# Three weight tiles for four in an expert's gate and up, and a down projection over 112 and 64 rows

## The chip, the cores and the metric

The kernel runs on one core of a Trainium2 chip. The metric is the device time of one execution in microseconds; the time before is the median of three runs, 1116.88 us (1115.35 to 1118.17). All data is float32.

## The reference

A transformer block with attention and a mixture of experts, on an input of 4 batches x 512 tokens x 256 features. Only the second half matters here; cut to it:

```python
h = layernorm(x) * (1 + cb) + sb                      # 2048 tokens x 256
scores = softmax(h @ gate.T)                          # 64 experts
# of 8 groups of experts the best 3 are kept, then the best 6 experts of a token
slot = expert * 96 + min(position_in_expert, 95)      # each expert has 96 places
buf[slot] = h[token]                                  # 64 x 96 x 256
g = einsum("ech,emh->ecm", buf, Wg)                   # Wg, Wu: 64 x 176 x 256
u = einsum("ech,emh->ecm", buf, Wu)
out = einsum("ecm,ehm->ech", silu(g) * u, Wd)         # Wd: 64 x 256 x 176
y = sum over a token's 6 places of out * weight
x = x + gb * (y + shared_expert(h))
```

So each of 64 experts takes a block of 96 tokens by 256 features through two matrices of 176 x 256 (gate and up), multiplies silu of one with the other, and goes back through one of 256 x 176.

## The kernel before

The kernel first computes attention (some 860 us), then routes each token and scatters its row, with its six weights, into the places of its experts in device memory (`slots_d`). The last stage, from about 916 to 1085 us, goes through the 64 experts; it is the only one that the change touches.

**Loads.** `load_pair(j)` (L719 to L727) fetches the weights of experts 2j and 2j+1: `wgu`, 128 partitions (one half of the features each time, index k) by expert, k, gate or up, and 176 columns; and `wd`, 88 partitions by expert, half m (2 x 88 = 176 rows of the down projection) and 256 columns, in two DMAs, of 80 and of 8 partitions. All are issued by SyncE (L722, L725, L726), three DMAs for a pair. `PAIRS` = 9 pairs of buffers exist; nine pairs are asked for ahead of the stage, and in the stage `load_pair` of a later pair is called after the down projection of an even expert, when its buffers come free. `load_group` (L733) fetches the tokens' rows `xe` of two experts, 96 partitions, through ScalarE's queue (the first four through SyncE's).

**One expert.** `features(e)` transposes the block of 96 x 256 in two halves (L825), and VectorE copies the result to `xT` (L827): 128 features by half and 96 tokens. `up(e)` makes gate and up: for gate and up, two tiles m of 88 weight columns, two halves k of the contraction, thus eight products with 96 streamed columns (L836), all into one PSUM bank. ScalarE takes silu of the gate (L839) into `act`, 88 partitions by m and token; VectorE multiplies it by the up half (L884). `down(e)` contracts those 88 rows twice (m = 0, 1) against `wd`, 256 streamed columns, into 96 x 256 (L847). ScalarE scales each token's row by its weight (L849, tile `oe`, six buffers), and GpSimd issues an indirect DMA that adds the rows to a sum in device memory (L850). There are four such sums (`NACC`); `sum_of(e)` picks one in turn, and from expert 48 (`EARLY`) only three of them, as the first is read early. DMAs into one sum wait for one another.

**Order.** The engines' programs follow the order in which the code issues them. The loop at L877 issues for each e: `up(e)`, `features(e+1)`, VectorE's product of expert e, and then `down(e-1)`; so TensorE has gate and up of expert e, the transposes of e+1, and the down projection of e-1, before gate and up of e+1. `weights_of` (L735 to L746, small VectorE operations on `xe`) is called every second expert, and from expert 56 VectorE also adds the first sum into the result (L869, L872).

**After the experts.** The shared expert of the last batch (`shared`, L755, L762) and its down projection (L768) run on TensorE while SyncE loads the three remaining sums (L909) as soon as they are complete. The last products (L957) add what a token gets from places that several tokens share, and the result is written out.

Earlier lines that are used for comparison: L136, L231 (projections of q, k and v), L267 and L327 (transposes), L422 (the router's product of 128 weight columns with 64 streamed columns), L526 (a transpose with 64 weight columns), L610 (modulation: four weight columns), L619 (transposes of four rows).

Of the kernel before, what the change touches and what calls it, by code (L numbers as in the profile page):

```python
# [8 lines left out]
F32 = mybir.dt.float32  # L9
I32 = mybir.dt.int32  # L10
U32 = mybir.dt.uint32
AF = mybir.ActivationFunctionType
# [5 lines left out]
P = 128  # L18
B, T, D = 4, 512, 256
NT = B * T  # L20
KC = D // P
# [7 lines left out]
E, M, CAP, TOPK = 64, 176, 96, 6  # L29
EG, TOPG = 8, 3  # L30
EPG = E // EG
MC, MP = 2, 88
MS = 352
MS_CHUNKS = [(0, 128), (128, 128), (256, 96)]
GA, SB, CB, GB = 0, 1, 2, 3
# [11 lines left out]
DW = 80  # L47
# [6 lines left out]
def adaln_attention_moe(ctx: ExitStack, tc: tile.TileContext, x, wq, wk, wv, wo, qkw, rope,  # L54
                        gate, wgu, wd, sgu, sd, c, wmod, out):
    nc = tc.nc
# [6 lines left out]
    def bank(tag):  # L63
        return psum.tile([P, 512], F32, tag=tag, name=f"ps_{tag}")
# [113 lines left out]
    with ExitStack() as att:  # L178
# [30 lines left out]
        def attention_input(b, pool=None, i0=0, n=NI, tag="tr"):  # L209

            pool = pool or rt
            xn = pool.tile([P, n, D], F32, tag=f"xn{i0}", name="xn")
            at = statistics(pool, b, i0, n)
            if n < NI:
                yield
            normalized(xn, b, *at, i0)
            yield
            for k in range(KC):
                nc.vector.tensor_scalar(hT[:, k, b * T + i0 * P:b * T + (i0 + n) * P], transposed(xn, k, tag),
                                        caT[:, k, b:b + 1], saT[:, k, b:b + 1], ALU.mult, ALU.add)  # L220
            yield
# [129 lines left out]
        second = {}  # L351
# [225 lines left out]
        halves = [attention_input(0, mp, i, 2, tag) for i, tag in ((0, "tr"), (2, "av"))]  # L577
# [4 lines left out]
        for j in range(4):  # L582
            for k in range(KC):
                nc.tensor.matmul(ps[:, j * B:(j + 1) * B], wm[:, k, j * P:(j + 1) * P], sil[:, k, :],
                                 start=(k == 0), stop=(k == KC - 1))
# [62 lines left out]
        for u in range(-HG, NU + 2):  # L648
            p, s, a, t = u + HG, u, u - 1, u - 2
# [58 lines left out]
    work = ctx.enter_context(tc.tile_pool(name="work", bufs=3, reuse_waits="tile"))  # L708
    held_weights = ExitStack()
    wexp = held_weights.enter_context(tc.tile_pool(name="w_exp", bufs=PAIRS, reuse_waits="tile"))  # L710

    sgu_sb = ffn.tile([P, KC, 2, MS], F32, name="sgu_sb")
    nc.sync.dma_start(out=sgu_sb, in_=sgu)
# [4 lines left out]
    pairs, groups = {}, {}  # L718

    def load_pair(j):  # L720
        a = wexp.tile([P, 2, KC, 2, M], F32, tag="wgu", name="wgu")
        nc.sync.dma_start(out=a, in_=wgu[2 * j:2 * j + 2].rearrange("e p k g m -> p e k g m"))  # L722
        d = wexp.tile([MP, 2, MC, D], F32, tag="wd", name="wd")
        src = wd[2 * j:2 * j + 2].rearrange("e p c d -> p e c d")
        nc.sync.dma_start(out=d[:DW], in_=src[:DW])  # L725
        nc.sync.dma_start(out=d[DW:], in_=src[DW:])  # L726
        pairs[j] = a, d  # L727

    def load_group(j, eng=nc.scalar):

        xe = work.tile([CAP, XB, ROW], F32, tag="xe", name="xe", bufs=XBUFS)
        groups[j] = [xe]
        return eng.dma_start(out=xe, in_=slots_d[j * XB * CAP:(j + 1) * XB * CAP, :].rearrange("(e c) r -> c e r", c=CAP))  # L733

    def weights_of(j):  # L735
        xe, = groups[j]
        w = work.tile([CAP, XB, TOPK], F32, tag="w", name="w", bufs=4)
        ids = expert_id[:CAP, j * XB:(j + 1) * XB].unsqueeze(2).to_broadcast([CAP, XB, TOPK])
        nc.vector.tensor_tensor(w, xe[:, :, ID0:ID0 + TOPK], ids, ALU.is_equal)
        nc.vector.tensor_mul(w, w, xe[:, :, W0:W0 + TOPK])  # L740
        w1 = work.tile([CAP, XB], F32, tag="w1", name="w1", bufs=4)
        nc.vector.tensor_reduce(w1, w, AX.X, ALU.add)
        nc.vector.tensor_tensor(w1, w1, low[:, j * XB:(j + 1) * XB], ALU.max)
        to = work.tile([CAP, XB], I32, tag="to", name="to", bufs=4)
        nc.vector.tensor_tensor(to, xe.bitcast(I32)[:, :, TOK], low_i[:, j * XB:(j + 1) * XB], ALU.max)
        groups[j] += [w1, to]  # L746
# [27 lines left out]
    def rows(t, b):  # L774

        return t[b * T:(b + 1) * T, :].rearrange("(p i) d -> p i d", p=P)
# [22 lines left out]
    for j in range(PAIRS):  # L799
        load_pair(j)  # L800
# [14 lines left out]
    def sum_of(e):  # L815

        return e % NACC if e < EARLY else 1 + e % (NACC - 1) if e < E - 1 else 2

    xTs, acts = {}, {}

    def features(e):
        xe = groups[e // XB][0]
        ps = bank("tr")
        for k in range(KC):
            nc.tensor.transpose(ps[:, k * CAP:(k + 1) * CAP], xe[:, e % XB, k * P:(k + 1) * P], ident[:CAP, :CAP])  # L825
        xTs[e] = work.tile([P, KC, CAP], F32, tag="xT", name="xT", bufs=2)
        nc.vector.tensor_copy(xTs[e].rearrange("p k c -> p (k c)"), ps[:, :KC * CAP])  # L827

    def up(e):
        a, xT = pairs[e // 2][0], xTs.pop(e)  # L830
        gu = bank("mm")
        guv = gu[:MP, :2 * MC * CAP].rearrange("p (g m c) -> p g m c", g=2, m=MC)
        for gi in range(2):
            for m in range(MC):
                for k in range(KC):
                    nc.tensor.matmul(guv[:, gi, m, :], a[:, e % 2, k, gi, m * MP:(m + 1) * MP], xT[:, k, :],  # L836
                                     start=(k == 0), stop=(k == KC - 1))
        act = acts[e] = work.tile([MP, MC, CAP], F32, tag="act", name="act", bufs=2)
        nc.scalar.activation(act, guv[:, 0], AF.Silu)  # L839
        return guv  # L840

    def down(e):
        d, act = pairs[e // 2][1], acts.pop(e)
        _, w1, to = groups[e // XB]
        po = bank("av")
        for m in range(MC):
            nc.tensor.matmul(po[:CAP, :D], act[:, m, :], d[:, e % 2, m, :], start=(m == 0), stop=(m == MC - 1))  # L847
        oe = work.tile([CAP, D], F32, tag="oe", name="oe", bufs=6)
        nc.scalar.activation(oe, po[:CAP, :D], AF.Copy, scale=w1[:, e % XB:e % XB + 1])  # L849
        nc.gpsimd.indirect_dma_start(out=y_d[sum_of(e)],  # L850
                                     out_offset=bass.IndirectOffsetOnAxis(ap=to[:, e % XB:e % XB + 1], axis=0),
                                     in_=oe, in_offset=None, compute_op=ALU.add)
# [4 lines left out]
    def load_shared_slots(eng, first, hi, step):  # L857
        eng.dma_start(out=o95[first:hi:step, :], in_=y_d[sum_of(first)][NT + first:NT + hi:step, :])
# [6 lines left out]
    def fold():  # L865

        for b in range(B):
            t = first_sums.pop(b)
            nc.vector.tensor_mul(t, t, gates(b))  # L869
            yield  # L870
            xb = x_sb[:, b * NI:(b + 1) * NI, :]
            nc.vector.tensor_add(xb, xb, t)  # L872
            yield

    weights_of(0)
    features(0)
    for e in range(E + 1):  # L877
        if e < E:
            if e % XB == 0 and 0 < e and e // XB + XBUFS - 1 < E // XB:
                load_group(e // XB + XBUFS - 1)  # L880
            guv = up(e)
            if e + 1 < E:
                features(e + 1)
            nc.vector.tensor_mul(acts[e], acts[e], guv[:, 1])  # L884
            if e % XB == XB - 1 and e + 1 < E:
                weights_of(e // XB + 1)
        if e >= 1:
            down(e - 1)
            if e % 2 == 0 and e // 2 + PAIRS - 1 < E // 2:
                load_pair(e // 2 + PAIRS - 1)  # L890
        if e == EARLY + 2:
            for b in range(B):
                first_sums[b] = wexp.tile([P, NI, D], F32, tag="wgu", name="first")
                nc.sync.dma_start(out=first_sums[b], in_=rows(y_d[0], b))
            folding = fold()
            load_shared_slots(nc.sync, 0, EARLY, NACC)
        if e > EARLY + 7:
            next(folding, None)
# [49 lines left out]
    for b in range(B):  # L948
        banks, to = kept if b == B - 1 else places(("av", "mm"), 2)
        w = NI // len(banks)  # L950
# [8 lines left out]
        for lo in range(0, NI, n):  # L959
            o = own[2][b][:, lo:lo + n, :]  # L960
# [63 lines left out]
```

## Time and profile before

| | |
|---|---|
| time, median of three runs | 1116.88 us |
| the profiled execution's time | 1117.43 us |
| its span, first to last instruction | 1115.7 us |
| mean granted TensorE clock | 0.992 |
| TensorE busy, share of the span | 97% |
| TensorE weight loads busy | 69% |
| VectorE, ScalarE, GpSimd busy | 58%, 40%, 37% |
| expert stage, first gate product to last down product | 917 to 1074 us |
| gate and up, L836: instructions, mean length | 1024, 250 ns |
| down, L847: instructions, mean length | 256, 383 ns |
| accumulating DMAs, L850: issue, median time to landing | 1.4 us, 7.7 us |
| DMA in 940 to 1040 us | 285 to 305 GB/s |

The page of the profile shows one execution. A row of a group gives line, engine, operation, the tiles written and read with their shapes, the count, the busy time in us and the mean length of one in ns, then the idle time before it and what ended it. For a matrix product the shape is rows x columns of the weight tile, then the operand that streams. "PEld" is the loading of weight tiles, which the profile lists beside the products. A row of waits reads: engine and operation, what it waited for, us in total, how often, the longest. A row of the timeline reads: start, length, engine, line, operation, tiles, shapes, how many were merged, and in brackets the idle time before. Ends of TensorE's products are modelled, so its starts say more than its lengths.

### The profile page before, as it was taken

The numbers are of one execution on the slowest core, as the hardware profiler recorded it, in microseconds if no ns is written. First come the engines' busy times: TensorE is split into PE (matmuls) and PEld (weight loads), VectorE is DVE, ScalarE is ACT, GpSimd is POOL, SyncE is SP. The second block draws the span as 40 slices with busy tenths as digits, with TensorE's granted clock in tenths as the row PEclk, the third lists the DMA queues.
The fourth block names the chain that finished last, engine by engine and source line by source line (L and its number), as shares of the span: only waits on it lengthen the run. The fifth ranks groups of instructions, "written<-read, shape, count | busy, mean of one in ns | idle before, by whom it ended". The sixth has DMA issues, their size and how long they took to land. (4 is left out here: it accounts for less than half of the span.)

```text
span 1115.7 us, 15635 instructions
## 1 busy us (share of the span) xinstructions
PE 1085.4 (97%) x5700; PEld 767.0 (69%) x5700; DVE 643.9 (58%) x1571; ACT 448.0 (40%) x741; POOL 417.7 (37%) x578
## 2 busy tenths in 40 slices
PE   9999999999999999999899999999999989999997
PEld 4567676667666766666667667666768659999966
DVE  5655655556667555567665556676544833444467
ACT  2553435344434453544444444535352412333320
POOL 3232223132223464323145632223562374565550
PEclk9999999999999999999999999999999998999999
DMA  5646404223101131110102220200122869999965
GB/s 191 227 114 183 161 12 149 78 84 104 57 20 63 49 112 67 40 56 21 57 30 97 77 88 9 68 1 30 60 89 88 229 221 244 303 297 289 264 140 200
DMA packets 67349, 130.20 MB, mean 117 GB/s; under 512 B 6564, under 2 KB 38852, under 8 KB 67144
## 3 DMA queue, kind: packets, MB, share of 16 engines
q1 hardware_dynamic: 48416, 102.49, 28.6%
q0 software_dynamic: 11776, 19.67, 7.1%
q10 hardware_dynamic: 7080, 7.04, 2.2%
q8 instruction: 45, 0.74, 0.3%
q14 instruction: 32, 0.26, 0.1%
HBM read 90.23 MB, written 38.94 MB: 116 GB/s over the span
## 5 line engine op out<-in xcount | busy, mean ns | idle before, releaser
L244 DVE TENSOR_REDUCE ss<-sq 128x4 f32<-128x512 f32 x128 | 87.2, 685 | 163.3 <-ACT sq L243 163.3
L145 POOL TENSOR_SCALAR rmsv<-ss 128x8 f32<-128x8 f32 x64 | 12.6, 198 | 448.2 <-DVE ss L244 448.2
L289 PE MATMUL ps_sc<-qT,kT 128*128 128x512 f32 (+3 forms) x512 | 158.1, 446 | 0.1
L314 PEld LDWEIGHTS ps_av<-v,es 128*128 128x128 f32 x1280 | 152.4, 192 | 3.0
L314 PE MATMUL ps_av<-v,es 128*128 128x129 f32 x1280 | 153.5, 275 | 0.0
L271 ACT COPY qT<-ps_tr 128x512 f32<-128x512 f32 x64 | 37.4, 585 | 267.1 <-PE ps_tr L267 267.1
L289 PEld LDWEIGHTS ps_sc<-qT,kT 128*128 128x128 f32 x512 | 87.2, 190 | 53.3 <-issue 31.3
L231 PE MATMUL ps_mm<-wk,hT 128*128 128x512 f32 x256 | 120.7, 594 | 0.7 <-ACT tokq L242 0.7
L231 PE MATMUL ps_mm<-wq,hT 128*128 128x512 f32 x256 | 120.6, 593 | 0.0
L231 PE MATMUL ps_mm<-wv,hT 128*128 128x512 f32 x256 | 120.6, 593 | 0.0
L338 PE MATMUL ps_mm<-wo,attnT 128*128 128x256 f32 x512 | 113.9, 380 | 4.8 <-DVE v L256 4.8
L850 POOL DMA_INDIRECT y_d<-oe,to x64 | 95.3, 1489 | 62.1 <-ACT oe L849 45.8
L292 ACT ACTIVATE es<-ps_sc 128x512 f32<-128x512 f32 (+1 forms) x192 | 99.9, 526 | 37.7 <-PE ps_sc L289 31.3
L338 PEld LDWEIGHTS ps_mm<-wo,attnT 128*128 128x128 f32 x512 | 96.9, 190 | 24.9 <-issue 6.7
L357 POOL DMA_INDIRECT slots_d<-row,to x96 | 95.5, 995 | 34.4 <-issue 15.5
L146 POOL TENSOR_TENSOR rmsr<-rmsv,mhalf 128x8 f32<-128x8 f32 x64 | 105.5, 1648 | 5.3
L836 PEld LDWEIGHTS ps_mm<-xT,wgu 128*88 128x88 f32 x1024 | 96.7, 161 | 9.1 <-issue 1.1
L836 PE MATMUL ps_mm<-xT,wgu 128*88 128x96 f32 x1024 | 98.2, 250 | 1.2 <-issue 0.7
L252 DVE TENSOR_TENSOR tokq<-tokq,rmsr 128x512 f32<-128x512 f32 x64 | 45.2, 706 | 89.6 <-POOL rmsr L146 89.6
L231 PEld LDWEIGHTS ps_mm<-wk,hT 128*128 128x128 f32 x256 | 48.3, 190 | 62.9 <-issue 57.2
L242 ACT COPY tokq<-ps_mm 128x512 f32<-128x512 f32 x64 | 37.5, 586 | 124.4 <-PE ps_mm L231 124.4
L294 ACT ACTIVATE es<-es 128x1280 f32<-128x1280 f32 x64 | 81.3, 1271 | 2.0
(207 smaller groups left out, 1502.3 us busy)
## 6 DMA issues: line engine op xcount, KB each, us to landing
wgu<-in_wgu SPq DMA_DIRECT2D x32, 704.0 KB
wd<-in_wd SPq DMA_DIRECT2D x32, 320.0 KB
y_d<-blank SPq DMA_DIRECT2D x4, 2304.0 KB
wq<-in_wq SPq DMA_DIRECT2D x16, 512.0 KB
wk<-in_wk SPq DMA_DIRECT2D x16, 512.0 KB
wv<-in_wv SPq DMA_DIRECT2D x16, 512.0 KB
wo<-in_wo SPq DMA_DIRECT2D x16, 512.0 KB
slots_d<-blank SPq DMA_DIRECT2D x1, 6528.0 KB
```

What stands on the lines that cost most here:

```text
L146: nc.gpsimd.tensor_tensor(r, v, mhalf[:, :n], ALU.pow)
L231: nc.tensor.matmul(ps, hT[:, k, lo:lo + P], weights[n, name][:, k, :], start=(k == 0), stop=(k == KC - 1))
L244: nc.vector.tensor_reduce(ss[:, j * HG:(j + 1) * HG], sq.rearrange("p (h d) -> p h d", d=HD), AX.X, ALU.add)
L252: nc.vector.tensor_mul(tv, tv, r[:, j * HG:(j + 1) * HG].unsqueeze(2).to_broadcast([P, HG, HD]))
L289: nc.tensor.matmul(ps[:, at:at + T - j * P], kT[:, j * P:(j + 1) * P], qT[:, j * P:], start=True, stop=True)
L292: nc.scalar.activation(es[:, base[js[0]]:base[js[0]] + at], ps[:, :at], AF.Tanh, scale=HD ** -0.5 / SOFTCAP)
L294: nc.scalar.activation(es[:, :1280], es[:, :1280], AF.Exp, scale=SOFTCAP)
L314: nc.tensor.matmul(pv[:, i2, :], es[:, lo:lo + P], v_tiles[n % 2][:, j, h, :], start=(j == 0), stop=(j == i))
L338: nc.tensor.matmul(ps[:, :D], attnT[n][:, h, i * P:(i + 1) * P], weights[n, "o"][:, h, :], start=(h == 0), stop=(h == HG - 1))
L357: d = nc.gpsimd.indirect_dma_start(out=slots_d, out_offset=bass.IndirectOffsetOnAxis(ap=to, axis=0), in_=rows, in_offset=None)
L836: nc.tensor.matmul(guv[:, gi, m, :], a[:, e % 2, k, gi, m * MP:(m + 1) * MP], xT[:, k, :], start=(k == 0), stop=(k == KC - 1))
L850: nc.gpsimd.indirect_dma_start(out=y_d[sum_of(e)], out_offset=bass.IndirectOffsetOnAxis(ap=to[:, e % XB:e % XB + 1], axis=0), in_=oe, in_o ...
```

## The change

Gate and up take the 176 columns as 112 + 64. Three weight tiles are used for four: gate's first 112 columns, a joined tile of 128 columns with the last 64 of gate and the last 64 of up, and up's first 112. The joined tile does not lie together in `wgu`, so VectorE copies those columns of a pair of experts to a new tile `wgc` (`join(j)`, two buffers): once ahead of the loop for pair 0, then after the multiplications of every even expert for the pair that comes next.

The products land in three pieces of 96 columns of the bank; the middle one has gate's last 64 on partitions 0 to 63 and up's last 64 on 64 to 127. ScalarE takes silu in two operations, VectorE multiplies in two. The second part of `act` goes to partitions 0 to 63 for even experts and 64 to 127 for odd ones (`second_chunk`).

The down projection contracts 112 rows, then 64 rows. The weights for it are two tiles: `wd1`, 112 partitions for both experts, and `wd2`, 128 partitions, the even expert's 64 rows above the odd one's. The array in device memory is as before (88 rows by two halves), so `wd1` takes 80 and 8 rows of the first half and 24 of the second, and `wd2` 64 rows of the second half, for each expert: five DMAs of rows of 256 elements, where there were two of rows of 512. With `wgu`, a pair is loaded in six DMAs.

```diff
+MA, MB = 112, 64
...
     def load_pair(j):
         a = wexp.tile([P, 2, KC, 2, M], F32, tag="wgu", name="wgu")
         nc.sync.dma_start(out=a, in_=wgu[2 * j:2 * j + 2].rearrange("e p k g m -> p e k g m"))
-        d = wexp.tile([MP, 2, MC, D], F32, tag="wd", name="wd")
+        d1 = wexp.tile([MA, 2, D], F32, tag="wd1", name="wd1")
+        d2 = wexp.tile([P, D], F32, tag="wd2", name="wd2")
         src = wd[2 * j:2 * j + 2].rearrange("e p c d -> p e c d")
-        nc.sync.dma_start(out=d[:DW], in_=src[:DW])
-        nc.sync.dma_start(out=d[DW:], in_=src[DW:])
-        pairs[j] = a, d
+        nc.sync.dma_start(out=d1[:DW], in_=src[:DW, :, 0])
+        nc.sync.dma_start(out=d1[DW:MP], in_=src[DW:, :, 0])
+        nc.sync.dma_start(out=d1[MP:], in_=src[:MA - MP, :, 1])
+        for e2 in range(2):
+            nc.sync.dma_start(out=d2[second_chunk(e2), :], in_=src[MA - MP:, e2, 1])
+        pairs[j] = [a, d1, d2]
+
+    def join(j):
+
+        a = pairs[j][0]
+        c = work.tile([P, 2, KC, 2, MB], F32, tag="wgc", name="wgc", bufs=2)
+        nc.vector.tensor_copy(c.rearrange("p e k g m -> p (e k g) m"), a.rearrange("p e k g m -> p (e k g) m")[:, :, MA:])
+        pairs[j].append(c)
+
+    def second_chunk(e):
+
+        return slice(e % 2 * MB, (e % 2 + 1) * MB)
...
     def up(e):
-        a, xT = pairs[e // 2][0], xTs.pop(e)
+        (a, _, _, c), xT = pairs[e // 2], xTs.pop(e)
         gu = bank("mm")
-        guv = gu[:MP, :2 * MC * CAP].rearrange("p (g m c) -> p g m c", g=2, m=MC)
-        for gi in range(2):
-            for m in range(MC):
-                for k in range(KC):
-                    nc.tensor.matmul(guv[:, gi, m, :], a[:, e % 2, k, gi, m * MP:(m + 1) * MP], xT[:, k, :],
-                                     start=(k == 0), stop=(k == KC - 1))
-        act = acts[e] = work.tile([MP, MC, CAP], F32, tag="act", name="act", bufs=2)
-        nc.scalar.activation(act, guv[:, 0], AF.Silu)
-        return guv
+        g, both, u = (gu[:, at * CAP:(at + 1) * CAP] for at in range(3))
+        halves = ((g[:MA, :], a[:, e % 2, :, 0, :MA]), (both, c[:, e % 2].rearrange("p k g m -> p k (g m)")),
+                  (u[:MA, :], a[:, e % 2, :, 1, :MA]))
+        for o, w in halves:
+            for k in range(KC):
+                nc.tensor.matmul(o, w[:, k, :], xT[:, k, :], start=(k == 0), stop=(k == KC - 1))
+        act = acts[e] = work.tile([P, 2, CAP], F32, tag="act", name="act", bufs=2)
+        second = second_chunk(e)
+        nc.scalar.activation(act[:MA, 0, :], g[:MA, :], AF.Silu)
+        nc.scalar.activation(act[second, 1, :], both[:MB, :], AF.Silu)
+        return (act[:MA, 0, :], u[:MA, :]), (act[second, 1, :], both[MB:, :])
 
     def down(e):
-        d, act = pairs[e // 2][1], acts.pop(e)
+        (_, d1, d2, _), act, second = pairs[e // 2], acts.pop(e), second_chunk(e)
         _, w1, to = groups[e // XB]
         po = bank("av")
-        for m in range(MC):
-            nc.tensor.matmul(po[:CAP, :D], act[:, m, :], d[:, e % 2, m, :], start=(m == 0), stop=(m == MC - 1))
+        nc.tensor.matmul(po[:CAP, :D], act[:MA, 0, :], d1[:, e % 2, :], start=True, stop=False)
+        nc.tensor.matmul(po[:CAP, :D], act[second, 1, :], d2[second, :], start=False, stop=True)
...
+    join(0)
     weights_of(0)
     features(0)
     for e in range(E + 1):
...
-            guv = up(e)
+            products = up(e)
             if e + 1 < E:
                 features(e + 1)
-            nc.vector.tensor_mul(acts[e], acts[e], guv[:, 1])
+            for g, u in products:
+                nc.vector.tensor_mul(g, g, u)
+            if e % 2 == 0 and e + 2 < E:
+                join(e // 2 + 1)
```

## The prediction

> **What bounds the kernel now.** I read the page first (TensorE busy 97% of the span), then the table of TensorE's waits in the expert stage, then its order of work there, then the end of the stage on GpSimd. The waits of PE from 900 to 1085 us:
>
> ```profile
> PE ps_tr L825 <- DMA xe<-slots_d: 2.3, 1, 2.3
> PE ps_mm L836 <- issue: 0.7, 1, 0.7
> PE ps_mm L836 <- DVE xT L827: 0.5, 1, 0.5
> PE ps_tr L768 <- DVE hs L762: 0.2, 1, 0.2
> ```
>
> There is no wait for a weight tile (`wgu`, `wd`) and none for an activation. So through 64 experts the PE order itself sets the pace. One expert of the timeline (start, length, engine, line; lengths overlap because ends are modelled, so read the starts):
>
> ```profile
> 950.62 0.33 PE L825 MATMUL ps_tr<-ident,xe 96*128 96x96 f32 x2
> 950.79 1.03 PE L847 MATMUL ps_av<-wd,act 88*96 88x256 f32 x4
> 951.47 1.51 PEld L836 LDWEIGHTS ps_mm<-xT,wgu 128*88 128x88 f32 x16
> 951.66 1.49 PE L836 MATMUL ps_mm<-xT,wgu 128*88 128x96 f32 x16
> 952.98 0.33 PE L825 MATMUL ps_tr<-ident,xe 96*128 96x96 f32 x2
> ```
>
> Starts give 0.17 us for the transposes, 0.87 for the down projection (4 x 216 ns), 1.32 for gate and up (16 x 82.5 ns): 2.36 per expert. A matrix product of float32 is two instructions here (16 for 8 products). The loads run beside the products, at the same pace.
>
> The end of the kernel hangs on something else. ScalarE's last result tile, then GpSimd's last accumulating DMAs:
>
> ```profile
> 1072.87 0.47 ACT L849 ACTIVATE oe<-ps_av,w 96x256 f32<-96x256 f32 x1 [0.57 <-PE ps_av L847]
> 1074.34 1.41 POOL L850 DMA_INDIRECT y_d<-oe,to  x1 [0.30 <-issue]
> 1076.06 1.41 POOL L850 DMA_INDIRECT y_d<-oe,to  x1 [0.30 <-issue]
> 1078.40 1.41 POOL L850 DMA_INDIRECT y_d<-oe,to  x1 [0.93 <-DMA y_d<-oe,to]
> ```
>
> The last tile is ready at 1073.34 and goes out at 1078.40: 5.1 us late, against 0.3 in mid-stage. Accumulations into one sum wait for one another, and from expert 48 there are three sums instead of four. So TensorE is followed by a short backlog, and a small slowing of TensorE would first only empty it.
>
> **Gate and up.** Twelve instructions replace sixteen, but the weight tiles grow from 88 columns to 112 and 128, while 96 columns are streamed as before. If streaming set the pace, 4 x 82.5 ns x 64 = 21 us would go. The trace has a row for the opposite case, the router's product: 128 weight columns, 64 streamed.
>
> ```profile
> 871.48 1.00 PE L422 MATMUL ps_mm<-gate_sb,hT 128*128 128x64 f32 x8
> 871.49 0.86 PEld L422 LDWEIGHTS ps_mm<-gate_sb,hT 128*128 128x128 f32 x7 [0.24 <-issue]
> ```
>
> (0.86 - 0.19) / 6 = 112 ns from load to load: loads set the pace there. A load of 88 columns lasts 157 ns (median, L836), one of 128 columns 192 (L422): 0.875 ns per column, so a load of 112 paces at 112 - 14 = 98 ns, one of 88 at 77 (below 82.5, which is why streaming rules now). New gate and up: 8 x 98 + 4 x 112 = 1232 ns of loads, less the first, which hides under the down projection's 216 ns, plus the last stream of 82: 1.216 us. Saving 0.104 us per expert, 6.7 us in all, not 21.
>
> Here the Trainium skill (TensorE: Matmul & The Clock Gate, Part 3, The mechanism) says otherwise: a weight load overlaps products in flight only if it goes to another row group. Then each instruction would pay load plus stream (80), 16 x 157 = 2.51 us now and 8 x 178 + 4 x 192 = 2.19 after: 20 us gained. The trace shows 16 loads of all 128 rows in 1.51 us beside 16 products in 1.49, so I take the row.
>
> **Down.** Still four instructions of 256 streamed columns, 216 ns each; fewer or more rows change nothing in the count. But the second product contracts 64 rows. The skill (TensorEngine Tiling (Array Packing), Key Properties) says that a change of tiling mode drains TensorE, and lists 64x128 as a mode of its own. Every expert would change twice: into it within the down projection, and back for the next gate and up. What a change costs is to be seen early in the trace, where L610 has a weight tile of four columns between full ones:
>
> ```profile
> 21.76 0.38 PE L267 MATMUL ps_tr<-ident,tokk 128*128 128x128 f32 x2
> 22.07 3.60 PE L610 MATMUL ps_av<-wm,sil 128*4 128x512 f32 x8
> 25.60 1.98 PE L231 MATMUL ps_mm<-wv,hT 128*128 128x512 f32 x4
> 27.42 1.88 PE L231 MATMUL ps_mm<-wq,hT 128*128 128x512 f32 x4
> 25.59 0.30 PEld L231 LDWEIGHTS ps_mm<-wv,hT 128*128 128x128 f32 x2 [0.86 <-issue]
> ```
>
> In: L267's last product starts at 21.76 + 0.38 - 0.27 = 21.87, the next is due 0.11 later, and comes at 22.07: +0.09. Out: L610's last starts at 25.08, the next is due at 25.51 and comes at 25.60: +0.09; its load began only then, uncovered, and the four products take 1.98 instead of 1.88: +0.10. So a change costs 93 ns plus the first load, which is no longer hidden. The four-row transposes (L619, 31.8 us) show the same both ways. Against it stands L526, with 64 weight columns:
>
> ```profile
> 845.04 0.60 PE L526 MATMUL ps_tr<-ident,share 128*64 128x128 f32 x4
> 845.48 0.60 PE L327 MATMUL ps_tr<-ident,attn 128*128 128x128 f32 x4
> ```
>
> 0.44 us for four, no gap, no loss. That is a transpose in float32, for which the same page (Restrictions) excludes column tiling, so it need not be a mode at all. Bounds for the two changes: nothing (as L526) and, as L610, 93 + 84 (a load of 96 columns) and 93 + 98 = 368 ns. I take 368: L526 alone is of the other kind. Net per expert 368 - 104 = +264 ns; times 64, less the last way out, +16.7 us at TensorE. By L526 it is -6.7.
>
> **What follows at the end.** At 2.62 us per expert the backlog goes: with weight loads over, three accumulations take 6.2 to 7.7 us (1058.28, 1064.47, 1072.12, 1078.40), 2.2 per expert. During the loads it is 9.1 for three (1042.43 to 1051.49), 3.0, but expert 48 then comes at about 1052, and the last pair of weights, issued at 1038, lands near 1046. So the last accumulation goes out 16.7 - 4.8 = 11.9 us later. The final products (L957) wait 1.5 us for DMA now; TensorE alone was ready at 1092.9. It arrives 16.7 later less the 2.3 us that L768 waits for `hs` (held up on VectorE by a sum that will now come early relative to it): 1107.3, against 1106.4 for the DMA side. So +12.9 us, +15.2 if that wait stays.
>
> **Beside the path.** VectorE copies 512 columns per pair (nearest rows, copies of 128x512 from PSUM at L256 and L328: 0.69; it can't be dearer by much) and multiplies twice (two of about 0.25 for 0.34); ScalarE activates twice (about +0.17). In 921 to 1040 us they are busy 46 and 39 of 119 us, and the `xT` copy, next on VectorE behind this copy, waits 84 us in 60 times for TensorE, 1.4 each: cover for 0.69. Without it a pair would lose up to 0.7 us. The copy reads the next pair's `wgu` one expert early; queued behind a late one would be `xT`, then TensorE. But the last pair landed at 1046.3 and is used at 1067.0, the tightest of all. `wd` goes in runs of 1 KB for 2 KB: packets of these sizes take 46 and 84 ns (medians), (352 x 46 - 176 x 84) / 16 = 0.09 us per pair on each DMA engine, 2 us over 22 pairs, within those 20.7. SyncE issues six DMAs per pair for three, some 1.05 us more of the 4.7 us per pair, where it is busy 1.04. All this I cost at nothing.
>
> **Sum.** 1117.43 + 12.9 = 1130.3 for the profiled execution, which lies 0.55 above the median: **1129.8 us**. Its own range, from drains of 300 ns to the `hs` wait kept and the copy sometimes uncovered, is 1123 to 1136.
>
> **Rivals.** (1) No drain for 64 rows (0.18): faster side. TensorE gains 6.7 us, but accumulations come four apart in 9.1 to 9.6 us when they queue (1025.79 to 1035.40, 1028.99 to 1038.07), 2.3 to 2.4 per expert, slower than TensorE's 2.25: the gain partly becomes backlog. Between 0 and -6.7, -3.5: 1113.4. It decides if the two changes cost under 104 + 4.8 / 64 x 1000 = some 180 ns, half of L610's. (2) The drain without uncovered loads (0.10): 186 - 104 = 82 ns, 5.2 us, nearly all of it taken by the backlog: 1117 to 1120. (3) Streaming sets the pace after all, and no drain: -21 us at TensorE, stopped by the accumulations at about 2.3 per expert, again near 1113; L422 speaks against it, and I count it within (1).
>
> Drain in full: 0.72. A difference under 0.3% (3.4 us) can't be told from no change here. Slower: 0.72 + half of (2) = 0.77; same: half of (2) and half of (1), 0.14; faster: half of (1), 0.09. The range that holds 8 in 10 runs from 1113.5 (half of rival 1 left out) to 1136.
>
> **What would show it.** Right: in the stage PE's two 64-row products start about 0.39 us after the 112-row ones instead of 0.22, the first gate load starts after, not with, the last down product; loads at 98 and 112 ns; 2.6 us per expert; POOL's lag 0.3 at the end. Wrong: loads under the last down product, 2.25 us per expert, and a lag over 5 us; or PE waits for `act`, `xT` or `wgu`, which I excluded.

## The result and the profile after

The change made the kernel slower: a median of 1148.72 us (1144.8 to 1154.45, four runs) against 1116.12 (1109.82 to 1118.17, four runs) for the kernel before, a ratio of **1.0306 [1.0245, 1.0367]** (ratios here and below are estimated from all runs of both kernels; the two medians alone give 1.0292). The forecast was 1129.8, with a range to 1136. The profiled execution of the changed kernel took 1144.8 us, with a span of 1143.0; it is the fastest of the four, so the median lies 3.9 us above what is accounted for here. (The granted clock was 0.988 in it and 0.981 to 0.983 in the others; every trace here has the clock at full or at half, so that 0.007 less over 1145 us is an estimated 16 us more at half, which could cost up to 8 us; the other three have no profile to show it.)

In the changed kernel the transposes are on L841, gate and up on L853, silu on L856 and L857, the down projection on L864 (112 rows) and L865 (64 rows), the result tile on L867, its accumulation on L868. The weights of a pair are issued on L723 (`wgu`) and L727 to L731, the token rows on L749, the loads of the first sum on L916, and its addition to the result is on L887 (multiplication) and L890.

**One expert.** This part went as forecast. Timeline of the changed kernel (start, length, engine, line, operation):

```profile
951.52 0.33 PE L841 MATMUL ps_tr<-ident,xe 96*128 96x96 f32 x2
951.69 0.60 PE L864 MATMUL ps_av<-wd,act 112*96 112x256 f32 x2
952.22 0.24 PEld L865 LDWEIGHTS ps_av<-wd,act 64*96 64x96 f32 x2 [0.36 <-issue]
952.22 0.67 PE L865 MATMUL ps_av<-wd,act 64*96 64x256 f32 x2
952.82 0.47 PEld L853 LDWEIGHTS ps_mm<-xT,wgu 128*112 128x112 f32 x4 [0.36 <-issue]
952.82 0.63 PE L853 MATMUL ps_mm<-xT,wgu 128*112 128x96 f32 x4
953.29 0.61 PE L853 MATMUL ps_mm<-xT,wgc 128*128 128x96 f32 x4
953.73 0.56 PE L853 MATMUL ps_mm<-xT,wgu 128*112 128x96 f32 x4
954.13 0.33 PE L841 MATMUL ps_tr<-ident,xe 96*128 96x96 f32 x2
```

From transposes to transposes it is 2.60 us (2.602 is also the median from expert to expert), where it was 2.36 (2.355). Both places where the row count changes are in it: the loads of L865 and of the first L853 start at the same time as their products, each after 0.36 us without a load. The two instructions of L865 fill 0.60 us, not 2 x 0.216 = 0.43. The start of the first comes 307 ns after the last 112-row product's (216 would be due), the first gate product comes 306 after the last 64-row one. From the middle tile's first product to the next tile's first is 0.44 us for four instructions, some 112 ns each for the tile of 128 columns; the last tile, of 112 columns, takes 0.40 us up to the transposes, some 98 ns each.

**The waits of TensorE.** From 900 to 1115 us:

```profile
PE ps_mm L853 <- issue: 13.5, 2, 12.9
PE ps_tr L841 <- DMA xe<-slots_d: 3.3, 1, 3.3
PE ps_mm L853 <- DVE xT L843: 0.5, 1, 0.5
```

The first row is new: one wait of 12.9 us, where the kernel before had none above 2.3. The row gives no cause ("issue"). The timeline around it does:

```profile
1071.89 0.67 PE L865 MATMUL ps_av<-wd,act 64*96 64x256 f32 x2
1076.43 1.11 SPq L731 DMA_DIRECT2D wd<-in_wd  x2
1077.71 4.66 SPq L916 DMA_DIRECT2D first<-y_d  x4
1083.73 1.22 DVE L887 TENSOR_TENSOR first<-first,mods 128x1024 f32<-128x1024 f32 x1 [13.62 <-DMA first<-y_d]
1084.98 0.36 DVE L843 COPY xT<-ps_tr 128x192 f32<-128x192 f32 x1
1085.44 1.03 PE L853 MATMUL ps_mm<-xT,wgu 128*112 128x96 f32 x4 [12.88 <-issue]
```

Read it from below. TensorE's gate product of expert 58 stood for 12.88 us. It needs `xT` from VectorE (L843), and VectorE stood for 13.62 us at L887, the instruction ahead of that copy in its program: the first piece of adding the first sum to the result, due at expert 56. Its tile was still being loaded: SyncE issued the load (L916) only at 1077.71, right behind the last weights of the last pair (L731). The same two instructions in the kernel before, with no wait ahead of the multiplication:

```profile
1042.20 5.53 SPq L894 DMA_DIRECT2D first<-y_d  x4
1055.13 1.22 DVE L869 TENSOR_TENSOR first<-first,mods 128x1024 f32<-128x1024 f32 x1
```

The loads are now 35 us later, and TensorE is only about 15 us later.

**SyncE's waits**, from 920 to 1080 us (what waited, for what; us in total, times, longest):

```profile
SPq L731 <- DMA xe<-slots_d: 25.6, 6, 6.3
SPq L727 <- DMA xe<-slots_d: 19.4, 6, 7.1
...
SPq L728 <- DMA xe<-slots_d: 6.2, 3, 5.5
```

A load of weights waits here for a load of token rows, which it neither reads nor overwrites and which another engine (ScalarE) issues. One such case in the queues of SyncE and of ScalarE:

```profile
1030.83 0.53 SPq L723 DMA_DIRECT2D wgu<-in_wgu  x1
1038.51 0.32 SPq L727 DMA_DIRECT2D wd<-in_wd  x1
```

```profile
1031.10 0.31 ACTq L749 DMA_DIRECT2D xe<-slots_d  x1
```

SyncE stands for 7 us inside a pair, until rows have landed whose load ScalarE had issued at 1031.10. A semaphore is a counter through which one part of the chip tells another that something is done. In the program as compiled, the DMAs of SyncE and ScalarE take the same eight semaphores in turn, and each may be issued only when the one eight places before it, on whichever of the two queues, has landed. (The trace records the semaphore with each issue: here L727 at 1038.51 waits for the one that the row load of 1031.10 had taken. The DMAs of GpSimd take eight others.) ScalarE issues a row load only when its own program, which goes at TensorE's pace, comes to it. Laid side by side, the two programs of the changed kernel have (counted from 0) pair 14 waiting for row loads 9 and 10, pair 17 for 13 and 14, pair 20 for 17 and 18, pair 23 for 21 and 22, pair 26 for 25 and 26, pair 30 for 31: about four row loads for three pairs. One row load is issued for every two experts, so three pairs take the time of eight experts: 8 x 2.602 / 3 = 6.94 us for a pair. Measured from the issue of the 10th pair's `wgu` to the last one's: (1073.85 - 923.01) / 22 = **6.86 us**. The kernel before took (1038.00 - 923.53) / 22 = 5.20.

The DMA engines had room: from 921 to 1067 us they moved 233 GB/s, where the kernel before moved 284 from 921 to 1040.

**The ledger**, from TensorE's starts in the two profiled executions:

| | before | after | difference |
|---|---|---|---|
| start to first gate product | 916.98 | 916.73 | -0.25 |
| first gate product to the shared expert (L755, now L771) | 155.64 | 187.09 | +31.45 |
| from there to the end of the span | 43.08 | 39.18 | -3.90 |
| span | 1115.7 | 1143.0 | +27.3 |

Of the 31.45, the wait is 12.88. After it TensorE ran at a granted clock of 0.50 for some 4 us, as the windows from 1085 us show (us, busy time of PE, PEld, DVE, ACT, POOL with counts, then granted clock, DMA share and GB/s):

```profile
1085.00:1087.00 2.00, 1.56 (x8) 1.59 (x9) 1.83 (x9) 0.00 (x0) 0.00 (x0) 0.50 0.51 200
1087.00:1089.00 2.00, 2.00 (x10) 1.47 (x9) 1.33 (x4) 0.38 (x2) 0.00 (x0) 0.50 0.00 1
```

From an expert's first gate product to the first 64-row product it was 3.74 us there (1085.44 to 1089.18) and 2.00 just before the wait (1069.89 to 1071.89): another 1.74. There remain 31.45 - 12.88 - 1.74 = 16.8 us for the slower TensorE. Of these, 1.55 us fell on the first three experts, where the granted clock was 0.50 until 928.7 in this execution and until 926.2 in the one before; the rest is 0.247 us for each later expert. The third line of the ledger, -3.90, holds the waits of TensorE that are gone from the end of the kernel (4.7 us before: 2.5 for `hs`, 1.5 for DMA, 0.7 for `own`). The backlog of accumulations is shorter: the last result tile (ready at 1104.45) goes out at 1107.15, 2.7 us later, not 5.1.

```profile
1103.98 0.47 ACT L867 ACTIVATE oe<-ps_av,w 96x256 f32<-96x256 f32 x1 [0.73 <-PE ps_av L865]
1107.15 1.41 POOL L868 DMA_INDIRECT y_d<-oe,to  x1 [1.83 <-ACT sg L776]
```

So the forecast's own terms came out at 16.8 - 3.9 = 12.9 us, as forecast, and 14.6 us came from a wait that it did not have. That they agree to 0.1 us is partly luck, as the first three experts show.

### The profile page after: what moved, and what is told of

It is laid out like the page before. It is cut to its first block, busy times and chain, and to the rows that moved or that the text cites. A ratio compares the mean times of both kernels' runs of the same rounds, so it can differ in the third digit from the quotient of the medians.

```text
span 1143.0 us, 15433 instructions
## 1 busy us (share of the span) xinstructions
PE 1101.5 (96%) x5444; PEld 751.6 (66%) x5444; DVE 670.9 (59%) x1667; ACT 454.5 (40%) x805; POOL 415.3 (36%) x578
## 5 line engine op out<-in xcount | busy, mean ns | idle before, releaser
L868 POOL DMA_INDIRECT y_d<-oe,to x64 | 93.8, 1465 | 92.7 <-ACT oe L867 70.6
L853 PE MATMUL ps_mm<-xT,wgu 128*112 128x96 f32 x512 | 79.3, 280 | 14.0 <-issue 13.5
L853 PEld LDWEIGHTS ps_mm<-xT,wgu 128*112 128x112 f32 x512 | 63.2, 185 | 37.2 <-issue 36.4
```

The source lines that it names most:

```text
L853: nc.tensor.matmul(o, w[:, k, :], xT[:, k, :], start=(k == 0), stop=(k == KC - 1))
L868: nc.gpsimd.indirect_dma_start(out=y_d[sum_of(e)], out_offset=bass.IndirectOffsetOnAxis(ap=to[:, e % XB:e % XB + 1], axis=0), in_=oe, in_o ...
```

## The experiments

**Theory.** Two things add up: the change to a 64-row product and back in every expert (about +1.4%), and the late loads of the first sum. These are late because six DMAs for a pair, sharing eight semaphores with the token rows, tie the weights' loads to TensorE's pace. **Rivals:** the loads follow TensorE whatever their number; or it is SyncE's own issue time and the smaller packets. In these kernels line numbers shift by a few. The kernel before ran beside each group of runs, with medians of 1113.78 to 1118.63, so ratios are compared.

**1. Three DMAs for a pair** (the weights lie in device memory as they are used, in two arrays).

```diff
-        src = wd[2 * j:2 * j + 2].rearrange("e p c d -> p e c d")
-        nc.sync.dma_start(out=d1[:DW], in_=src[:DW, :, 0])
-        nc.sync.dma_start(out=d1[DW:MP], in_=src[DW:, :, 0])
-        nc.sync.dma_start(out=d1[MP:], in_=src[:MA - MP, :, 1])
-        for e2 in range(2):
-            nc.sync.dma_start(out=d2[second_chunk(e2), :], in_=src[MA - MP:, e2, 1])
+        nc.sync.dma_start(out=d1, in_=wd1[2 * j:2 * j + 2].rearrange("e p d -> p e d"))
+        nc.sync.dma_start(out=d2, in_=wd2[j])
```

> The changed kernel with the down weights laid out by the host as 112 and 128 rows, so that a pair is loaded in three DMAs instead of six; packets stay 1 KB, TensorE's program stays as it is. Theory (two causes: about 16 us of tiling changes on TensorE, and about 13 us of one VectorE wait for the first sum's tiles, which come late because six DMAs per pair hold one another up through their semaphores): the wait in the fold vanishes, the expert keeps 2.60 us, and the time falls by 12 to 15 us, to about 1134. Rival (the 1 KB packets or the DMA engines themselves are what makes the loads late): nothing vanishes, 1145 to 1150.

1132.5 us, 1.0123 [1.0076, 1.0171]. An expert still takes 2.602 us, a pair 5.34. SyncE's queue at the end of the loads:

```profile
1045.51 0.33 SPq L727 DMA_DIRECT2D wd<-in_wd  x1
...
1050.37 7.27 SPq L912 DMA_DIRECT2D first<-y_d  x3
```

The first sum's loads begin 27 us sooner than in the changed kernel, and the multiplication at 1071.57 does not wait. SyncE's waits (920 to 1060 us) show no token rows; it now waits for buffers that TensorE still reads:

```profile
SPq L726 <- PE ps_av L860: 22.0, 7, 5.6
```

By the semaphores in the trace, the row loads 6 to 26 now take two of the eight in turn and wait only for one another: three weight DMAs and one row load make four, which divides eight, so no weight load shares a semaphore with a row load from pair 11 on. With the loads out of the way, what is left is the forecast: 1.0123 on 1116.88 would be 1130.6.

**2. No change of row count, six DMAs kept**: the second product runs over all 128 rows, and the half of `act` that belongs to the other expert holds zeros.

```diff
+    act_of = [work.tile([P, 2, CAP], F32, tag=f"act{i}", name=f"act{i}", bufs=1) for i in range(2)]
+    for i in range(2):
+        nc.gpsimd.memset(act_of[i][(1 - i) * MB:(2 - i) * MB, 1, :], 0.0)
...
-        nc.tensor.matmul(po[:CAP, :D], act[second, 1, :], d2[second, :], start=False, stop=True)
+        nc.tensor.matmul(po[:CAP, :D], act[:, 1, :], d2, start=False, stop=True)
```

> The changed kernel with the second down product contracted over all 128 rows, the other expert's 64 rows of act being zero, so that no product has 64 rows; six DMAs per pair stay. Theory: TensorE needs 2.23 to 2.25 us per expert where nothing is late, but the loads still take their own pace, near 6.9 us per pair, so the first sum's tiles land near 1085 as before and TensorE waits longer for them: 1135 to 1142, some 10 us under the changed kernel. Rival (the loads' pace follows TensorE's, since their semaphores are shared with transfers that TensorE releases): the loads speed up with it, and most of the wait goes too, 1118 to 1128.

1128.73 us, 1.0083 [1.0057, 1.0109]: neither the theory's figure nor quite the rival's. An expert takes 2.252 us, so the whole cost of the row change is gone. But the wait stays, in the waits of TensorE and of VectorE:

```profile
PE ps_mm L856 <- issue: 18.4, 2, 12.7
```

```profile
DVE first L890 <- DMA first<-y_d: 11.7, 1, 11.7
```

The rival is right in one thing, which the theory had missed: the loads got faster with TensorE, 5.90 us for a pair. By the four-for-three rule it should be 8 x 2.252 / 3 = 6.0. The loads and TensorE keep the same ratio, so a faster TensorE meets the same late sum. (This kernel's stage also began 7 us later: its first gate product waited 5.6 us at 924; why was not followed up.)

**3. Both.**

> Both edits together: no product of 64 rows, three DMAs per pair. Theory: neither cause is left; TensorE 2.23 us per expert, and the accumulations into four and three sums, at 2.3 us per expert, hold back part of it: 1110 to 1115, that is 0.1 to 0.6% under the kernel before. Rival (the third weight tile, the joining copies or the doubled activations cost something of their own): 1118 or more.

1114.84 us, 0.9964 [0.9943, 0.9985], 2.252 us for an expert. TensorE's order of work without the row change:

```profile
1019.62 0.59 PE L863 MATMUL ps_av<-wd,act 112*96 112x256 f32 x2
1020.06 0.60 PE L864 MATMUL ps_av<-wd,act 128*96 128x256 f32 x2
1020.49 0.54 PE L852 MATMUL ps_mm<-xT,wgu 128*112 128x96 f32 x4
1020.87 0.61 PE L852 MATMUL ps_mm<-xT,wgc 128*128 128x96 f32 x4
1021.31 0.56 PE L852 MATMUL ps_mm<-xT,wgu 128*112 128x96 f32 x4
```

Down takes 4 x 216 ns again, and gate and up 1.22 us (1020.49 to 1021.71, the next transposes), 0.10 less than the 1.32 before: the forecast's saving. It does not all arrive, for the eight semaphores work in the other direction too. ScalarE stood for 5.4 us ahead of its silu, because the row load in front of it in its program waited for a weight load:

```profile
1035.15 0.34 ACTq L745 DMA_DIRECT2D xe<-slots_d  x1
1035.59 0.25 ACT L855 ACTIVATE act<-ps_mm 112x96 f32<-112x96 f32 x1 [5.38 <-DMA wd<-in_wd]
1036.31 1.17 PE L863 MATMUL ps_av<-wd,act 112*96 112x256 f32 x2 [3.02 <-DVE act L903]
```

**4. Six DMAs in the kernel before**: its `wd` is loaded in five pieces.

```diff
-        nc.sync.dma_start(out=d[:DW], in_=src[:DW])
-        nc.sync.dma_start(out=d[DW:], in_=src[DW:])
+        nc.sync.dma_start(out=d[:DW, :, 0], in_=src[:DW, :, 0])
+        nc.sync.dma_start(out=d[DW:, :, 0], in_=src[DW:, :, 0])
+        nc.sync.dma_start(out=d[:24, :, 1], in_=src[:24, :, 1])
+        for e2 in range(2):
+            nc.sync.dma_start(out=d[24:, e2, 1], in_=src[24:, e2, 1])
```

> The kernel before with its down weights loaded in the five pieces of the changed kernel (1 KB runs) into its old tile: six DMAs per pair, TensorE's program untouched. Theory: the loads fall to about 6.9 us per pair, the first sum's tiles land some 25 us later than before and VectorE, then TensorE, waits: 1130 to 1142. Rival (six DMAs are hidden, and what made the changed kernel slow is all on TensorE): 1116 to 1119.

1119.85 us, 1.0008 [0.9989, 1.0026]: **the theory missed.** Six DMAs alone are all but hidden. The end of SyncE's loads and VectorE's wait show how nearly:

```profile
1055.31 1.15 SPq L729 DMA_DIRECT2D wd<-in_wd  x2
1057.85 3.83 SPq L897 DMA_DIRECT2D first<-y_d  x4
```

```profile
DVE first L872 <- DMA first<-y_d: 0.8, 1, 0.8
```

A pair took 5.59 us (5.20 before), the sum's loads came 16 us later than before, and its multiplication at 1063.3, 5.5 us after the issue. VectorE stood 0.8 us for it, where in the changed kernel it stood 13.6, and TensorE lost nothing there. (It lost 2.4 us in two other places, where ScalarE's silu came late behind a row load that waited for weights, as in 3.) In this kernel's program pair 31 waits for row load 28, where in the changed one pair 30 waits already for 31: the same eight semaphores, but the two queues meet in another order, with less to wait for. Why the order comes out so differently was not settled. The number of DMAs is therefore not the cause by itself; the order in which they meet the row loads should be. The next experiment takes the row loads out of that order.

**5. Token rows through GpSimd's queue**, in the changed kernel, all six DMAs kept:

```diff
-    def load_group(j, eng=nc.scalar):
+    def load_group(j, eng=nc.gpsimd):
```

> The changed kernel with the expert's token rows loaded through GpSimd's queue instead of ScalarE's, so that they no longer take turns with the weight loads on the eight semaphores that SyncE's and ScalarE's transfers share; six DMAs per pair, their packets and TensorE's program stay. Theory (a weight load waits for a transfer of token rows that stands eight places before it and that is issued only when TensorE gets there): the first sum's tiles land some 20 us earlier, the wait in the fold goes, 1130 to 1137. Rival (six DMAs cost by themselves: issue time on SyncE, or small transfers on the DMA engines): 1142 to 1150.

1129.29 us, 1.0135 [1.0118, 1.0152], a pair in 5.38 us. SyncE's waits (920 to 1060 us) and its queue:

```profile
SPq L727 <- PE ps_av L864: 49.3, 23, 5.4
```

```profile
1044.92 1.11 SPq L731 DMA_DIRECT2D wd<-in_wd  x2
1049.13 12.56 SPq L916 DMA_DIRECT2D first<-y_d  x4
```

No wait for `xe` is left, and the sum's multiplication at 1070.40 does not stand. One word changed, and 1.7 points of the 3.1 went. SyncE issues as many DMAs as in the changed kernel, with packets as small, so its issue time and the packets are out as the cause. The same edit in the kernel before is the control:

> The kernel before with only its token rows loaded through GpSimd's queue. It tells what of the 0.5% that the version with all three edits gained is the change itself. If the three weight tiles bring it: 1 (within 0.2%) of the kernel before, since TensorE waited for nothing there. If the queue brings it: 0.995 to 0.997.

1120.68 us, 1.0014 [0.9997, 1.003]. The queue brings nothing of itself. It even takes a little: here the first sum's loads go out at 1048.73, 6.5 us later than before, and VectorE stands for them.

```profile
DVE first L869 <- DMA first<-y_d: 2.8, 1, 2.8
```

TensorE stands for 1.8 us behind it, so in the kernel before too this tile has little to spare.

**6. The first sum added later**, in the changed kernel:

```diff
-        if e > EARLY + 7:
+        if e > EARLY + 13:
```

> The changed kernel with the first step of the fold (the multiplication that waits for the first sum's tiles) issued from expert 62 on instead of 56; the steps that are left over come after the loop. Loads and TensorE's program unchanged. Theory (TensorE stands still only because VectorE's in-order queue stops at the fold): the tiles land near 1082 as before, expert 62 is reached at about 1083, so the standstill of 12.9 us goes and 1133 to 1140 is left, some of it for the folds after the loop. Rival (late weights would have stopped TensorE anyway a little later): 1143 or more.

1139.01 us, 1.0234 [1.0214, 1.0254]. The standstill is gone; TensorE's longest wait is again 3.4 us, for the first token rows. The stage is 10.8 us shorter than in the changed kernel (176.3 for 187.1), but what follows it is 4.9 longer (44.1 for 39.2), as part of the additions now comes after the experts. In this execution TensorE also had half its clock until 938.2 (928.7 in the changed kernel), which made the first five experts 3.9 us longer; without that the stage would be 14.7 us shorter, close to the 14.6 of the wait and its half clock. So the late tile is what stopped TensorE, and to wait for it later is only half a cure. The rival was that late weights would stop TensorE anyway. Weights did come late here, at the joining copies of the last two pairs, but TensorE didn't wait for it:

```profile
DVE wgc L738 <- DMA wgu<-in_wgu: 1.6, 2, 1.2
```

**7. The row change alone**, in the kernel before: the second product contracts 64 of its 88 rows, so that 24 of an expert's 176 rows are left out of the sum.

```diff
-            nc.tensor.matmul(po[:CAP, :D], act[:, m, :], d[:, e % 2, m, :], start=(m == 0), stop=(m == MC - 1))
+            nc.tensor.matmul(po[:CAP, :D], act[:64 if m else MP, m, :], d[:64 if m else MP, e % 2, m, :], start=(m == 0), stop=(m == MC - 1))
```

> The kernel before with one edit: the second down product contracts 64 of its 88 rows (24 rows of each expert's 176 are left out of the sum), two rows of instructions as before. Nothing else differs, so this is the price of going into a 64-row product and back. Theory: 93 us/1000 of emptying plus an uncovered load, both ways, and the first gate product after it stretched: 0.33 us per expert, 21 us, less the 4.8 us of backlog that it empties: 1130 to 1136. Rival (64 rows alone cost little, the 0.25 us per expert of the changed kernel come from the wider loads or the waits for two halves of act): 1116 to 1122.

1129.28 us, 1.0143 [1.0126, 1.0159], +15.5 us. The timeline shows the two loads that no longer hide:

```profile
950.33 0.24 PEld L847 LDWEIGHTS ps_av<-wd,act 64*96 64x96 f32 x2 [0.36 <-issue]
950.93 1.39 PEld L836 LDWEIGHTS ps_mm<-xT,wgu 128*88 128x88 f32 x16 [0.36 <-issue]
950.93 1.55 PE L836 MATMUL ps_mm<-xT,wgu 128*88 128x96 f32 x16
```

An expert takes 2.684 us, 0.33 more than 2.355, with nothing else of the change. Backlog at the end: 1.5 us for 5.1.

**8. A version faster than both**: three DMAs, 128 rows with zeros, token rows through GpSimd's queue.

> Both edits (no 64-row product, three DMAs per pair) and the token rows through GpSimd's queue. In the run with both edits ScalarE once stood 5.4 us before issuing token rows, waiting for a weight transfer's semaphore. Theory: that standstill goes, 1108 to 1114. Rival (GpSimd's longer queue makes the accumulations late by as much, since the kernel's end hangs on them): 1115 to 1122.

> The version with all three edits again, beside the control on the same chip: three weight tiles, no 64-row product, three DMAs per pair, token rows through GpSimd's queue. Expected again 0.993 to 0.997 of the kernel before.

The second is the same kernel again. 1108.78 us, 0.995 [0.9932, 0.9968], and then, on another chip, 1111.42, 0.9925 [0.9902, 0.9949]. So the three weight tiles are worth 0.5 to 0.75% once they neither change the row count nor delay loads. (What the new layout of the down weights in device memory would do for the kernel before was not measured.)

| kernel | us for an expert | us for a pair's loads | ratio to before |
|---|---|---|---|
| before | 2.355 | 5.20 | 1 |
| changed | 2.602 | 6.86 | 1.0306 |
| three DMAs | 2.602 | 5.34 | 1.0123 |
| rows by GpSimd | 2.602 | 5.38 | 1.0135 |
| no row change | 2.252 | 5.90 | 1.0083 |
| both | 2.252 | 4.79 | 0.9964 |
| both, rows by GpSimd | 2.252 | 4.73, 4.86 | 0.995, 0.9925 |
| before with six DMAs | 2.355 | 5.59 | 1.0008 |
| before, rows by GpSimd | 2.355 | 5.31 | 1.0014 |
| before with the row change | 2.684 | 5.56 | 1.0143 |

The row change costs 1.6 points with three DMAs and 2.2 with six; the DMAs cost 1.8 points with the row change and 1.2 without.

## Why the prediction was wrong

**Gate and up: right.** Paces of 98 and 112 ns were forecast from L422's row, and both were measured; the saving of 0.104 us for an expert is 2.355 - 2.252 = 0.103 where nothing else disturbs it. The rule that loads overlap only with products of another row group (the Trainium skill, TensorE: Matmul & The Clock Gate, Part 3, The mechanism) fails here as it did before: four loads of 128 columns pass in 0.45 us beside their products. (The same section also lets a load go ahead when it targets a background weight buffer; the forecast left that out.)

**Down: right.** 368 ns were forecast for the two changes, and 264 net of the saving; the net was 2.602 - 2.355 = 0.247. The changed kernel against "both" gives 2.602 - 2.252 = 0.350, and the change alone, with an 88-column load on the way out, 0.33. The step from four weight columns (L610) to 64 rows held. The skill's rule (TensorEngine Tiling (Array Packing), Key Properties) that another tiling mode drains the array fits these rows; about 0.09 us each way is the emptying, the rest is the load that can't hide.

**The end: right in sum.** +16.7 at TensorE and -3.8 from the two waits at the end (2.3 for `hs`, 1.5 for the last accumulation) were forecast; +16.8 and -3.9 were measured, the first with some luck: the pace alone is 64 x 0.247 = 15.8, and a longer half clock at the start of the stage made up the rest. With the rows on GpSimd's queue, where no standstill disturbs the sum, the same two terms are +16.7 and -4.0 (and half the clock lasted until 929.0). The backlog did not empty quite to 0.3 us: the last tile was 2.7 late, as it stood behind a wait of another kind on GpSimd (the timeline names `sg` of the shared expert), and 1.2 with the rows on GpSimd's queue.

**Beside the path: wrong.** This is the step that failed: "SyncE issues six DMAs per pair for three, some 1.05 us more of the 4.7 us per pair, where it is busy 1.04. All this I cost at nothing", and ahead of it "But the last pair landed at 1046.3 and is used at 1067.0, the tightest of all". The term put at nothing was a wait of 12.9 us and its after-effect of 1.7. Three things were left out.

- A DMA was costed by its issue time and its bytes, not by what it has to wait for. The sign was in the kernel before, in SyncE's waits from 920 to 1060 us:

```profile
SPq L725 <- DMA xe<-slots_d: 16.7, 4, 5.0
...
SPq L722 <- DMA xe<-slots_d: 11.3, 3, 5.1
```

  A load of weights that waits for token rows on another engine's queue has no reason in the data; something is shared. With its third row (L726, 7.8 us) that is 36 us in nine times; in the changed kernel it is 57 us in seventeen, up to 1080 us, and there they set the pace. (The bytes were rightly held cheap: the median packet of 1 KB on SyncE's queue takes 46 ns in the changed kernel, and the weights' packets of 2 KB took 98 before, not the 84 of the forecast, so 352 for 176 cost nothing.)
- What is queued behind the weights on SyncE was not followed. The weights themselves were not waited for in the changed kernel, though narrowly: pair 29's `wgu` landed at 1067.0 and the joining copy read it at 1069.7. With the sum added later (6.) the copies of the last two pairs waited. Behind them stand the first sum's loads, and those had, before, 12.9 us from issue (1042.20) to use (1055.13). By the semaphore records of the trace the first piece landed at 1050.5: 4.6 us to spare, not the 20.7 taken for "the tightest of all". (By the same records the last pair's `wgu` landed at 1047.4, not 1046.3. And 4.7 us for a pair is TensorE's pace; the loads took 5.20.)
- The one user of that tile stands in VectorE's queue in front of `xT`, so that TensorE stops with it. The forecast looked at what a late `wgu` would hold up through this queue, but not at the addition of the sum. A wait for `xT` was on its list of signs of being wrong, and that is what came.

Measured, the missing term is 12.88 us of standstill and 1.74 of half clock after it. The profiled execution: 1117.43 + 12.9 + 14.6 = 1144.9, measured 1144.8. The list of rivals had no mechanism of this kind. What remained of the forecast is the time with three DMAs or with the rows on another queue: 1.0123 and 1.0135, 1130.6 and 1132.0 us on the 1116.88 before.

**Rival 1** (no cost of the 64 rows, faster) was wrong about the chip, but right about what a kernel without that cost would gain: it gave -6.7 us at most, and the last version is, by the medians, 5.0 and 7.2 us faster than the kernel before beside it.

**VectorE and ScalarE: right.** The joining copy takes 0.416 us, less than the 0.69 allowed for it, and TensorE waited for none of it in the changed kernel; two multiplications of 0.25 and two silu of 0.25 hide as forecast.

**Open.** Shown is that the standstill goes with fewer DMAs, with the rows on another queue, or with the sum added later. Not shown is why the compiled order sets pair 30 behind row load 31 in the changed kernel, and pair 31 behind 28 in the kernel before with six DMAs, nor why runs of the changed kernel differ by up to 0.8%; the three longer ones had the lower granted clock.

## What to carry to other kernels

Before a load is split into more DMAs at no cost, look in the waits of the issuing queue for a wait on a transfer that has nothing to do with it: that is a shared resource, and every added DMA moves the point at which the two queues meet. Follow each queue past the edited instructions to what stands behind them and who needs that next, and price the shortest of these covers, not the one of the edited tile. If the rows left over are as few as the 64 here (112 cost nothing extra), fill the product up with zeros rather than contract fewer: the 128-row product took 216 ns per instruction, as the one over 88 rows had, and the two changes in every expert went.

## What the hardware did that was not expected

- Contracting 64 rows between taller products cost 0.33 us for the way in and the way out together, and was foreseen only from four weight columns elsewhere in the trace. The same product over 128 rows, half of them zeros, took 216 ns per instruction and cost nothing around it.
- After 12.9 us without work TensorE was granted half its clock for about 4 us, so that the standstill cost 1.74 us beyond its own length. The clock had fallen within it, at 1075.5, and came back at 1089.1; without the row change the same followed the wait of 12.7 us (half clock from 1060.7 to 1074.4).
- The DMA engines moved less (233 for 284 GB/s) while the loads were late: here a falling rate was a sign of transfers that were not issued, not of a full memory.
- VectorE's copy of 128x512 within SBUF took 0.416 us, where those from PSUM take 0.69.
